# Scores of the plain block placed directly behind it, in layer one of a two-layer graph attention

## The chip, the cores and the metric

The kernel runs on one core of one Trainium2 chip. The core has a matrix engine (TensorE, PE in the profile, its weight loads PEld), VectorE (DVE), ScalarE (ACT), GpSimd (POOL), and DMA queues, of which most here are issued by SyncE (SP). The metric is the time on the device of one execution, as the median of several.

## The reference, cut to what matters

```python
h = jnp.maximum(_layernorm(x, axis=-1), 0.0)          # x: (128, 64, 768)
for l in range(2):
    m_left  = einsum('bsh,oh->bso', h, W_left[l])
    m_right = einsum('bsh,oh->bso', h, W_right[l])
    u_left  = einsum('bih,bjh->bij', h, m_left) / sqrt(768)
    u_right = einsum('bih,bjh->bij', h, m_right) / sqrt(768)
    u = u_left * triu(adj) + u_right * swapaxes(triu(adj, 1), 1, 2)
    e = exp(u) * adj
    attention = e / (sum(e, axis=2) + 1e-10)
    ctx = attention @ (einsum('bsh,oh->bso', h, W_lin[l]) + b_lin[l])
    h = relu((ctx - mean) / (std + 1e-3) * ln_a[l] + ln_b[l])
return x + h
```

All matrices are 32-bit floats. What matters here are `m_left` and `m_right` (six blocks of 256 output columns in all, each a sum over three blocks of 256 input columns) and the scores, the products of `h` with them inside each batch of 64 tokens.

## The kernel before, in words

The 8192 tokens are cut into 32 parts of 256 tokens (four batches of 64). Each layer has two passes: `pass_one` makes `m_left`, `m_right`, the scores and the softmax, `pass_two` the rest. Only layer one's `pass_one` (in the code `l == 0`) is touched.

That pass starts with the **plain block**: parts 0 and 1, whose 12 output blocks (six per part) are made as 12 chains of three block products each, 36 in all. Behind it come the **superblocks** of three parts each (`SUPER[1]`, `SUPER[2]`, ...). A superblock needs only 40 block products (`PRODUCTS`, L116) for its 54 plain ones, by a bilinear scheme: each product multiplies a sum of weight blocks (`W_OPS`, L142) with a sum of token blocks (`T_OPS`, L133), and its result is added into several output blocks (`READS`, L122). Sums of weights are made once, while the plain block runs, on VectorE and GpSimd; sums of tokens are made anew for each superblock, on GpSimd. I call a weight sum W followed by its number in `W_OPS`, a token sum T followed by its number in `T_OPS`, and the first superblock's products 0, 1, 2, ... as they stand in `PRODUCTS`. Products 0, 1, 3, 4, 5, 6 and 7 take the token sums T9, T12, T16, T17, T19, T21 and T23.

A block product (`product`, L691) is four matmuls of 128x128 on 256 columns, which the profile lists as eight records. Its output fills one PSUM bank of 512 columns. Four banks take turns (`bank_of`): C, D, X, Y in the plain block and in the first superblock. There are six such banks (Z and V are the others), and two more, `sc`, that hold scores.

**Output of the plain block.** When a chain ends, ScalarE copies its bank into the output tile (L889): even chains belong to part 0 (tile `m0`), odd ones to part 1 (`m1`). The last four copies (chains 8 to 11) are, by bank, C, D, X and Y; chain 10 completes `m0`, and chain 11 `m1`.

**Staging.** While the plain block is emitted, `weights.stage` is a list of PSUM banks. A weight sum on VectorE first has one operand copied by ScalarE into the next bank of that list (L517), and then reads that bank and one SBUF tile (L522 or L245). The list is a ring: a bank can be filled again when the sum that read it has ended. In the first superblock the list is empty, and sums read SBUF alone. The copies of L517 and L889 share ScalarE's queue in the order in which they are emitted.

**Scores.** `scores(k)` (L722) makes the scores of superblock k: for each pair of batches q (two per part), for each of the six channel blocks c, four small matmuls; 96 matmuls or 192 records for the plain block. The first half reads `m0`, the second `m1`. Its output for the plain block is the first of the two `sc` banks, which is also the third bank of the staging ring. In the superblock behind it, it is emitted after product 3. The reads of products 0 to 3 overwrite the same `m` tiles and so come behind it.

**Softmax.** `softmax(k)` gives eight steps, put into the plan three slots apart (a product has two slots): masks on GpSimd (L745, tile `wm`), then VectorE work that reads the scores (L755), an exponential on ScalarE, and at last a transpose and eight DMAs of SP's queue (L778).

All engines work through their own queue in the order of emission. `turn_of(slot)` runs what the plan holds for a slot and emits sums by a planner's clock that counts slots, not microseconds.

Of the kernel before, what the change touches and what calls it, by code (L numbers as in the profile page):

```python
# [17 lines left out]
def kernel(  # L18
# [48 lines left out]
    def put(slot, *fs):  # L67
        plan.setdefault(slot, []).extend(fs)

    def put_all(slot, fs, step=1):  # L70
        for f in fs:
            if f is not None:
                put(slot, f)
            slot += step
        return slot
# [99 lines left out]
    SCORED = 3  # L175

    def begins(k, l=0):
        return 0 if k == 0 else 2 * (len(PRODUCTS) if l else PLAIN) + 2 * len(PRODUCTS) * (k - 1)
# [142 lines left out]
    KEEP = {}  # L321
# [333 lines left out]
    def pass_one(l, start, final):  # L655
        with tc.tile_pool(name=f"one{l}", bufs=2, reuse_waits="tile") as sp, \
# [34 lines left out]
            def product(bank, w, ts, new, slot, n=TH):  # L691
                p = bank[:, :2 * n].rearrange("p (g n) -> p g n", g=2)
                for g in range(2):
                    for c in range(K2):
                        at = 0
                        for t in ts:
                            t = t[:, c]
                            n = math.prod(t.shape[1:])
                            o = p[:, g, at:at + n]
                            if len(t.shape) == 3:  # L700
                                o = o.rearrange("p (b s) -> p b s", b=t.shape[1])
                            nc.tensor.matmul(o, w[:, c, g * P:(g + 1) * P], t,  # L702
                                             start=(new and g == c == at == 0), stop=(c == K2 - 1),
                                             skip_group_check=True)
                            at += n
                    if g == 0:
                        turn_of(slot)

            def out_of(bank, thirds=False, o=0):
                if thirds:  # L710
                    p = bank[:, :4 * CUT].rearrange("p (g b s) -> p g b s", g=2, s=WIDE)
                    return p[:, :, :, THIRDS[o // 6][1]:]
                return bank.rearrange("p (g b s) -> p g b s", g=2, s=S)

            def into(o, thirds=False):
                v, k, i = o // 6, o // 3 % 2, o % 3
                if thirds:
                    r, n = THIRDS[v]
                    return both[:, i * K2:(i + 1) * K2, :, k, r + n:r + WIDE]
                return M[v][:, i * K2:(i + 1) * K2, :, k, :]  # L720

            def scores(k):  # L722
                nq = 2 * len(SUPER[k])
                p = KEEP["scores"].rearrange("p a (q m) -> p (a q) m", m=P)
                for q in range(nq):
                    ht, m = HT[1, l, SUPER[k][q // 2]], M[q // 2]
                    for c in range(C):
                        for h in range(PAIR):
                            b = q % 2 * PAIR + h
                            mb = both[:, c, q // 2 * PB + b] if l and k == 0 else m[:, c, b]  # L730
                            mb = mb.rearrange("p k j -> p (k j)")
                            for e in (0, 32):
                                nc.tensor.matmul(p[h * S + e:h * S + e + 32, q, e:e + 95],  # L733
                                                 ht[:, c, b * S + e:b * S + e + 32], mb[:, e:e + 95],
                                                 start=(c == 0), stop=(c == C - 1))
# [45 lines left out]
            def softmax(k):  # L781
                CHAIN[k] = chain(k)
                return [lambda: next(CHAIN[k], None)] * 8

            mid = None
            if l == 0:
# [18 lines left out]
                def mid():  # L805
                    for f in turns[1:]:
                        f()
                    load_rows(0, 1, sp)
                    load_rows(0, 2, other)
                    for t in range(2):  # L810
                        nc.sync.dma_start(KEPT[0][t], HT[1, 0, t])
                    load_adj(0)
                    cols.extend([column("a_col", ln_a[0]), column("b_col", ln_b[0])])
# [8 lines left out]
            def bank_of(n):  # L822
                n %= BANKS
                return KEEP["CD"][n] if n < 2 else KEEP["XYZV"[n - 2]]

            weights, tokens = Weights(() if l else W_OPS, 2, True), TOKENS[l]
# [5 lines left out]
            def turn_of(slot):  # L832
                now = slot * 0.86 if l == 0 or slot >= 80 else slot * 0.6 + 20.8
                clock["vector"] = max(clock["vector"], now - 1.0) + sum(getattr(f, "vector", 0.0) for f in plan.get(slot, ()))
                run(slot)
                if fetch and slot >= start["weights"] and slot % 3 and free:
                    fetch.popleft()()
                if weights.left and slot >= start["weights"]:
                    while clock["vector"] <= now and weights.some(nc.vector):
                        clock["vector"] += 0.62  # L840
                    if clock["pool"] <= now and start["pool"] <= slot < start["tokens"]:
                        if weights.some(nc.gpsimd, 40):
                            clock["pool"] = max(clock["pool"], now) + 1.35
                if clock["pool"] <= now + 1.5 and tokens.step(slot):
                    clock["pool"] = max(clock["pool"], now) + 1.35
# [32 lines left out]
            slot = 0  # L878
            for n, (w, t) in enumerate(order):
                bank = bank_of(n % CHAINS)  # L880
                for j in range(3):
                    tok = HT[1, l, t][:, j * K2:(j + 1) * K2, :]
                    product(bank, weights.at[3 * w + j], [tok], j == 0, slot)
                    weights.used(3 * w + j)
                    if j == 2:
                        if n == 0 and mid:
                            mid()
                            weights.stage = [KEEP["Z"], KEEP["V"], KEEP["scores"][:, 0]]
                        nc.scalar.copy(into(6 * t + w), out_of(bank))  # L889
                    turn_of(slot + 1)  # L890
                    slot += 2
            weights.stage = []

            last = len(SUPER) - 1
            for k in range(FIRST_OF[l], len(SUPER)):
                assert slot == begins(k, l)
                if k:
                    put_all(slot + 2 * SCORED + 4, softmax(k - 1), 3)
                    put(slot + 2 * SCORED + 42, lambda k=k: load_adj(k, nc.scalar))
                if k == last:  # L900
                    final(slot, tokens)
                seen, waiting = set(), []

                def reads(i):
                    for o, c in READS[i]:
                        bank = out_of(bank_of(CHAINS * (k - 1) + i % CHAINS), k == 0, o)
                        to = into(o, k == 0)
                        if o not in seen:
                            seen.add(o)
                            nc.scalar.activation(to, bank, AF.Copy, scale=float(c))  # L910
                        elif abs(c) == 1:
                            added(nc.vector, to, "+" if c > 0 else "-", to, bank)
                        else:
                            nc.vector.scalar_tensor_tensor(to, bank, float(c), to, op0=ALU.mult, op1=ALU.add)  # L914

                for i, (f, t) in enumerate(PRODUCTS):
                    while l and f not in weights.at:
                        fetch.popleft()()
                    w, tok = weights.need(f), tokens.need(k, t)
                    product(bank_of(CHAINS * (k - 1) + i % CHAINS), w, tok, i < CHAINS, slot, TH if k else 2 * CUT)  # L920
                    tokens.used(k, t)
                    if k == last:
                        weights.used(f)
                    waiting.append(i)
                    if i == SCORED and k:
                        scores(k - 1)
                    if i >= SCORED or k == 0:
                        for n in waiting:
                            reads(n)
                        waiting = []  # L930
                    turn_of(slot + 1)
                    slot += 2
# [432 lines left out]
```

## Time and profile before

| | us |
|---|---|
| median of 3 runs | 2652.43 |
| lowest and highest | 2652.22, 2653.41 |
| the profiled execution | 2648.42 |
| its span, first to last instruction | 2646.6 |

TensorE was granted a mean of 0.995 of its full clock in the profiled execution. The plain block starts 11.18 us after the span's start, and the first superblock's product 0 at 77.08 us. In a timeline, a row gives the start, the duration, the engine, the line, the operation, the tiles (out<-in), how many instructions are merged, and in brackets how long the engine sat idle before and which instruction ended that.

### The profile page before, as it was taken

The numbers are of one execution on the slowest core, as the hardware profiler recorded it, in microseconds if no ns is written. First come the engines' busy times: TensorE is split into PE (matmuls) and PEld (weight loads), VectorE is DVE, ScalarE is ACT, GpSimd is POOL, SyncE is SP. The second block draws the span as 40 slices with busy tenths as digits, with TensorE's granted clock in tenths as the row PEclk, the third lists the DMA queues.
The fourth block names the chain that finished last, engine by engine and source line by source line (L and its number), as shares of the span: only waits on it lengthen the run. The fifth ranks groups of instructions, "written<-read, shape, count | busy, mean of one in ns | idle before, by whom it ended". The sixth has DMA issues, their size and how long they took to land. (4 is left out here: it accounts for less than half of the span.)

```text
span 2646.6 us, 47202 instructions
## 1 busy us (share of the span) xinstructions
PE 2591.6 (98%) x18122; PEld 2217.1 (84%) x18122; DVE 1780.6 (67%) x2888; ACT 935.4 (35%) x1969; POOL 1763.1 (67%) x1392
## 2 busy tenths in 40 slices
PE   9899999999999999999999999999999989999998
PEld 8788888888888888888798888888888878887886
DVE  7878787777768445554456667677666676666667
ACT  5522223223113244454542222122222335555453
POOL 4766676666668657676276666667666657878786
PEclk9999999999999999999999999999999999999999
DMA  7443534343421354445794424253532215555655
GB/s 220 113 111 86 124 93 110 93 119 79 98 60 56 123 156 149 159 139 182 219 282 101 121 68 108 71 129 93 136 98 70 67 49 157 157 167 166 177 161 146
DMA packets 258465, 331.84 MB, mean 125 GB/s; under 512 B 56002, under 2 KB 190402, under 8 KB 258242
## 3 DMA queue, kind: packets, MB, share of 16 engines
q1 hardware_dynamic: 241442, 320.56, 44.3%
q10 hardware_dynamic: 16800, 8.26, 1.2%
q8 instruction: 145, 2.38, 0.4%
q14 instruction: 78, 0.64, 0.1%
HBM read 213.39 MB, written 115.34 MB: 124 GB/s over the span
## 5 line engine op out<-in xcount | busy, mean ns | idle before, releaser
L245 POOL TENSOR_TENSOR g<-ht 128x512 f32<-128x512 f32 (+1 forms) x620 | 785.9, 1279 | 420.8 <-PE Z L702 71.6
L245 POOL TENSOR_TENSOR g<-g,g 128x512 f32<-128x512 f32 (+1 forms) x310 | 397.9, 1291 | 136.7 <-PE C L702 22.0
L245 POOL TENSOR_TENSOR g<-ht,g 128x512 f32<-128x512 f32 (+1 forms) x272 | 346.1, 1282 | 164.8 <-PE Z L702 42.8
L702 PE MATMUL X<-g,g 128*128 128x256 f32 (+1 forms) x1080 | 252.9, 377 | 6.0 <-DVE m L914 6.0
L1006 PE MATMUL Z<-g,g 128*128 128x256 f32 x1024 | 244.1, 380 | 3.5 <-ACT hl L300 3.2
L702 PE MATMUL C<-g,g 128*128 128x256 f32 x1008 | 239.7, 381 | 4.9 <-POOL g L245 2.2
L702 PEld LDWEIGHTS X<-g,g 128*128 128x128 f32 x1080 | 203.0, 191 | 34.8 <-DVE m L914 6.8
L702 PE MATMUL Y<-g,g 128*128 128x256 f32 (+1 forms) x968 | 225.7, 376 | 3.8 <-POOL g L245 3.8
L1006 PEld LDWEIGHTS Z<-g,g 128*128 128x128 f32 x1024 | 191.6, 190 | 35.8 <-issue 4.1
L379 ACT ACTIVATE ht<-ht,b_col,a_col 128x256 f32<-128x256 f32 x384 | 196.1, 591 | 69.0 <-DMA ht<-h 53.8
L702 PEld LDWEIGHTS C<-g,g 128*128 128x128 f32 x1008 | 190.5, 190 | 32.9 <-POOL g L245 3.5
L702 PE MATMUL Z<-g,g 128*128 128x256 f32 (+1 forms) x936 | 217.0, 375 | 0.0
L702 PE MATMUL D<-g,g 128*128 128x256 f32 x880 | 209.8, 381 | 1.8 <-POOL g L245 1.8
L702 PEld LDWEIGHTS Y<-g,g 128*128 128x128 f32 x968 | 182.0, 190 | 27.8 <-POOL g L245 4.2
L702 PE MATMUL V<-g,g 128*128 128x256 f32 (+1 forms) x840 | 194.6, 375 | 3.1 <-POOL g L245 1.6
L702 PEld LDWEIGHTS Z<-g,g 128*128 128x128 f32 x936 | 174.5, 190 | 23.1
L702 PEld LDWEIGHTS D<-g,g 128*128 128x128 f32 x880 | 168.1, 191 | 25.7 <-POOL g L245 2.5
L1006 PE MATMUL X<-g,g 128*128 128x256 f32 x768 | 182.7, 379 | 0.0
L702 PEld LDWEIGHTS V<-g,g 128*128 128x128 f32 x840 | 157.6, 191 | 23.3 <-POOL g L245 1.7
L1206 POOL TENSOR_TENSOR z<-z,b 128x768 f32<-128x768 f32 x62 | 112.7, 1829 | 81.7 <-DVE z L1203 77.2
L245 DVE TENSOR_TENSOR m<-m,Y 128x512 f32<-128x512 f32 (+2 forms) x196 | 126.5, 667 | 58.4 <-ACT m L910 35.7
L245 DVE TENSOR_TENSOR m<-m,D 128x512 f32<-128x512 f32 x180 | 118.2, 677 | 70.0 <-ACT m L910 51.3
(222 smaller groups left out, 4612.0 us busy)
## 6 DMA issues: line engine op xcount, KB each, us to landing
ht<-h SPq DMA_DIRECT2D x126, 768.0 KB, 6.3
h<-xb SPq DMA_DIRECT2D x124, 384.0 KB, 6.6
z<-z SPq DMA_DIRECT2D x128, 192.0 KB, 3.1
x<-z SPq DMA_DIRECT2D x128, 192.0 KB, 5.4
xr<-in_x_dram SPq DMA_DIRECT2D x120, 192.0 KB, 3.8
out_dram<-xr SPq DMA_DIRECT2D x120, 192.0 KB, 2.7
x<-in_x_dram SPq DMA_DIRECT2D x112, 192.0 KB, 5.4
g<-form SPq DMA_DIRECT2D x40, 256.0 KB, 5.6
```

The costliest lines, as they stand in the source:

```text
L245: (eng.tensor_add if sign == "+" else eng.tensor_sub)(o, a, b)
L379: nc.scalar.activation(ht, ht, AF.Relu, bias=cols[1][:, c:c + 1], scale=cols[0][:, c:c + 1])
L702: nc.tensor.matmul(o, w[:, c, g * P:(g + 1) * P], t, start=(new and g == c == at == 0), stop=(c == K2 - 1), skip_group_check=True)
L1006: nc.tensor.matmul(p[:, n], b[t][:, c, r * P:(r + 1) * P], w[s][:, c, :], start=(i in FIRST and i not in PRELOAD and n == c == 0), stop=(c ...
L1206: nc.gpsimd.tensor_add(zs[k], zs[k], rows["b"])
```

## The change

The scores of the plain block are emitted in front of product 0 instead of behind product 3. The reads of products 0 to 3 then follow each product at once. The softmax steps of the plain block start at slot 2 of the superblock instead of slot 10. As the scores' output is the third bank of the staging ring, the ring has only Z and V from chain 8 on. The conditions `l or k > 1` and `l + k` confine all that to layer one's first superblock; layer two and all later superblocks are emitted as before.

```diff
             for n, (w, t) in enumerate(order):
                 bank = bank_of(n % CHAINS)
+                if n == 8:
+                    weights.stage = [KEEP["Z"], KEEP["V"]]
                 for j in range(3):
...
             weights.stage = []
 
+            if not l:
+                scores(0)
             last = len(SUPER) - 1
             for k in range(FIRST_OF[l], len(SUPER)):
                 assert slot == begins(k, l)
                 if k:
-                    put_all(slot + 2 * SCORED + 4, softmax(k - 1), 3)
+                    put_all(slot + (2 * SCORED + 4 if l or k > 1 else 2), softmax(k - 1), 3)
...
                     waiting.append(i)
-                    if i == SCORED and k:
+                    if i == SCORED and l + k > 1:
                         scores(k - 1)
-                    if i >= SCORED or k == 0:
+                    if i >= SCORED or l + k < 2:
                         for n in waiting:
                             reads(n)
                         waiting = []
```

## Prediction

> **What bounds the kernel now.** The page first: TensorE is busy nearly throughout, so what a change of order can give lies in its gaps.
>
> ```profile
> span 2646.6 us, 47202 instructions
> PE 2591.6 (98%) x18122; PEld 2217.1 (84%) x18122; DVE 1780.6 (67%) x2888; ACT 935.4 (35%) x1969; POOL 1763.1 (67%) x1392
> ```
>
> Then the timeline of PE around the place:
>
> ```profile
> 69.55 5.34 PE L702 MATMUL Y<-ht,g 128*128 128x256 f32 x24
> 77.08 2.51 PE L702 MATMUL C<-g,g 128*128 128x256 f32 x8 [2.19 <-POOL g L245]
> 81.39 3.78 PE L702 MATMUL D<-g,g 128*128 128x256 f32 x8 [1.79 <-POOL g L245]
> 84.96 2.03 PE L702 MATMUL X<-g,g 128*128 128x256 f32 x8
> 90.80 2.57 PE L702 MATMUL Y<-g,g 128*128 128x256 f32 x8 [3.80 <-POOL g L245]
> 93.30 5.16 PE L733 MATMUL sc<-m,ht 128*32 128x95 f32 x192
> 99.49 1.97 PE L702 MATMUL C<-g,g 128*128 128x256 f32 x8 [1.04 <-ACT m L910]
> 101.30 1.89 PE L702 MATMUL D<-g,g 128*128 128x256 f32 x8
> 103.02 1.89 PE L702 MATMUL X<-g,g 128*128 128x256 f32 x8
> ```
>
> The last plain chain ends at 69.55 + 5.34 = 74.89. Product 4 starts at 99.49. Between lie products 0 to 3, the scores, and 2.19 + 1.79 + 3.80 + 1.04 = 8.8 us of idle time, most of it spent on token sums of GpSimd. From product 4 on products follow each other every 1.72 us. So the question is when product 4 starts; what it loses or gains there stays to the end, as PE sets the pace behind it.
>
> PE idles because the sums are late, and ScalarE shows by how much:
>
> ```profile
> 59.76 0.57 ACT L517 COPY sc<-g 128x512 f32<-128x512 f32 x1
> 73.99 0.59 ACT L517 COPY sc<-g 128x512 f32<-128x512 f32 x1 [0.23 <-DVE g L245]
> 81.97 0.58 ACT L889 COPY m<-X 128x512 f32<-128x512 f32 x1
> 87.94 0.58 ACT L889 COPY m<-Y 128x512 f32<-128x512 f32 x1
> 88.42 0.59 ACT L517 COPY sc<-g 128x512 f32<-128x512 f32 x1
> ```
>
> The copies of chains 10 and 11 (L889) stand in ScalarE's queue between staging copies, and those wait for VectorE. Chain 11 left PE at 74.89, and its copy starts at 87.94. Before, that is covered: the scores, which need it, come at 93.30. VectorE, which sets this pace, has no gap:
>
> ```profile
> 60.44 0.69 DVE L522 SCALAR_TENSOR_TENSOR g<-sc,g 128x512 f32<-128x512 f32 x1 [0.82 <-ACT sc L517]
> 68.08 0.68 DVE L245 TENSOR_TENSOR g<-Z,g 128x512 f32<-128x512 f32 x1
> 68.68 0.68 DVE L245 TENSOR_TENSOR g<-V,g 128x512 f32<-128x512 f32 x1
> 73.27 0.69 DVE L245 TENSOR_TENSOR g<-sc,g 128x512 f32<-128x512 f32 x1
> 74.09 0.69 DVE L522 SCALAR_TENSOR_TENSOR g<-Z,g 128x512 f32<-128x512 f32 x1
> 89.10 0.68 DVE L245 TENSOR_TENSOR g<-sc,g 128x512 f32<-128x512 f32 x1
> ```
>
> From 68.08 (the first staged sum emitted in chain 8, W77) to 89.10 (the last, W109) there are 33 sums, 32 steps in 21.02 us: 23 steps of 0.60 (68.08 to 68.68) and 9 of some 0.80 (73.27 to 74.09), the latter mostly where a sum reads or overwrites its predecessor's data.
>
> **The ring of two (first step).** With two banks, a bank's round is the sum (0.69), the way to ScalarE (73.27 + 0.69 = 73.96 to 73.99: 0.03), the copy (0.59) and the way back (59.76 + 0.57 = 60.33 to 60.44: 0.11): 1.42 us for two sums, 0.71 each, a little less where L245 reads the bank; I take 0.69. The 9 steps of 0.80 stay; the 23 of 0.60 cost 0.09 more, 2.07 us. Four plain copies hold ScalarE for 0.48 each (87.94 to 88.42), and a ring of two leaves it no lead to hide them; half of that, 1.0, I count. Together 3.0 us. Carried forward sum by sum with the same durations, three banks give the measured 87.94 and two give 84.3 for chain 10's copy and 90.9 for chain 11's, landing 0.58 later at 84.9 and 91.5. Bounds: nothing, if banks always come free in time; and, if each of the 32 steps takes the longest seen here, 0.82, and all four copies count in full, 26.2 + 1.9 - 21.0 = 7.1 us.
>
> **The scores in front (second step).** They need chain 10's copy for the first part and chain 11's for the second. How fine that wait is can be seen behind them:
>
> ```profile
> 98.27 1.08 ACT L910 ACTIVATE m<-C 128x512 f32<-128x512 f32 x2 [9.25 <-PE sc L733]
> ```
>
> This overwrites a middle third of `m1`, and starts before the scores end at 93.30 + 5.16 = 98.46; so waits go by pieces of a tile. Four of the six channel blocks of a batch pair need no late copy, which leaves three stretches: 32 records at once, 96 behind chain 10's copy, 64 behind chain 11's. Were waits by whole tiles, 96 would be behind the last.
>
> PE's clock matters here. These windows are cut where the granted clock (the column behind POOL) changes, 3.41 us apart:
>
> ```profile
> 74.98:78.39 3.41, 1.31 (x6) 1.18 (x7) 3.28 (x6) 2.97 (x6) 3.28 (x3) 1.00 0.98 334
> 78.39:81.80 3.41, 1.61 (x5) 0.82 (x4) 3.20 (x6) 3.32 (x7) 2.54 (x2) 0.50 1.03 239
> 81.80:85.22 3.42, 3.42 (x9) 2.70 (x9) 3.32 (x6) 3.40 (x7) 2.13 (x2) 0.50 1.04 220
> 85.22:88.63 3.41, 1.77 (x8) 1.22 (x7) 3.31 (x7) 3.18 (x7) 0.88 (x2) 1.00 0.48 103
> 88.63:92.04 3.41, 1.25 (x6) 1.12 (x7) 3.41 (x5) 0.39 (x1) 3.33 (x3) 1.00 0.03 7
> 92.04:95.46 3.42, 3.42 (x60) 2.68 (x62) 3.35 (x9) 0.00 (x0) 2.66 (x3) 0.50 0.01 2
> ```
>
> A window with PE busy for 1.31 or 1.25 us is followed by one at half clock, one with 1.77 is not, and a full one restores it. At half clock a product takes 84.96 - 81.39 = 3.57 us, 0.446 a record against 0.216. The scores by clock (the same view, L733 alone):
>
> ```profile
> 93.30:95.46 2.16, 2.16 (x56) 2.16 (x60) 0.50 0.01 4
> 95.46:98.46 3.00, 3.00 (x144) 2.78 (x136) 1.00 0.03 5
> ```
>
> That is 2.16 / 56 = 0.0386 us a record at half clock, and 3.00 / 136 (started there) = 0.0221 at full.
>
> **The sum.** From 74.9, 32 records take 0.7 us. PE then idles to 84.9, and by the windows its clock is halved. 96 records at 0.0386 last to 88.6, which fills a window, so the clock returns. Idle to 91.5; that window is busy for 0.5 us, so half clock comes at 92.04. 64 records: 22 until then, 42 at half, to 93.7. Product 0 runs 3.95 records until 95.46 and the other 4.05 at 0.216, to 96.3. Products 1 to 3 add 3 x 1.73. Product 4 starts at 101.5 against 99.49: **2.0 us later**. Without the ring's 3.0 it would be earlier, and the wait of 1.04 ahead of product 4 is already gone in this sum, since reads now follow each product.
>
> The Trainium skill speaks to this in "TensorE: Matmul & The Clock Gate", section "HAM oscillation — how this bites in real kernels": the throttle returns after gaps in PE's work of over some 3.4 us. By that, the gap from 88.6 to 91.5 would not halve the clock again, and product 4 would start at 91.5 + 64 x 0.0221 + 4 x 1.73 = 99.8. The trace disagrees: gaps of 2.19 and 1.79 us brought half clock at 78.39 and kept it.
>
> **What lies beside.** Rows that bear on the moved work:
>
> ```profile
> 88.13 2.61 POOL L245 TENSOR_TENSOR g<-ht,g 128x512 f32<-128x512 f32 x2 [2.53 <-DVE g L522]
> 97.26 1.43 POOL L745 TENSOR_TENSOR wm<-adj,tri 128x256 f32<-128x256 f32 x2
> ```
>
> T15 and T16 are the two of 88.13: T15's buffer comes free with a late weight sum (W115), so with the ring they end some 2.4 us later, and the masks (L745, 1.43 us), emitted ahead of T16 now, add to that: 90.7 + 2.4 + 1.4 = 94.5. Product 3 starts at 99.8; cover 5.3 us. T17 to T23 follow at some 1.3 each (2.61 / 2), and by that rate stand before their products by 2 us or more.
>
> ```profile
> 92.38 0.64 DVE L522 SCALAR_TENSOR_TENSOR g<-g,g 128x512 f32<-128x512 f32 x1
> 94.11 0.81 DVE L245 TENSOR_TENSOR g<-g,g 128x512 f32<-128x512 f32 x1
> 100.37 0.69 DVE L245 TENSOR_TENSOR m<-m,D 128x512 f32<-128x512 f32 x1 [4.27 <-ACT m L910]
> ```
>
> The moved reads add one wait on VectorE: product 1's read (100.37) now stands ahead of W116 (94.11), which so waits for product 1's end at 98.1 and, with the statistics between them, ends near 101. T21 takes the buffer that W116 frees, and would be there at 102 for product 6 at 105.0. Cover 3 us; beyond it PE waits.
>
> ```profile
> 118.30 5.16 SPq L461 DMA_DIRECT2D h<-xb  x4
> 123.63 9.47 SPq L361 DMA_DIRECT2D x<-in_x_dram  x8
> 133.22 5.73 SPq L778 DMA_DIRECT2D att<-wm  x8
> 139.06 1.00 SPq L368 DMA_DIRECT2D ht<-h  x2
> ```
>
> The eight attention DMAs are emitted eight slots earlier and so pass the stores and loads of 118.30 and 123.63, which come up to 5.7 us later. The load of 139.06 keeps its place, and its tokens are for superblock 2, some (152 - 80) / 2 x 1.73 = 62 us behind product 4, near 164. The softmax's own steps on VectorE and ScalarE come earlier into queues that wait for PE. I cost all this at nothing.
>
> **Against the runs.** In the profiled execution, of 2648.42 us with 2646.6 of span, this gives 2650.4; it is 4.0 below the median of the runs, 2652.43. The forecast is the median plus 2.0: **2654.4 us**. Its own range: 0.4 (clock never halved again) to 4.9 (whole-tile waits 1.2, a worse phase of the windows 0.7, the ring at 4.0), 2652.8 to 2657.3.
>
> **Rivals.**
>
> *The gate stays open* behind the first scores. +0.4, **2652.8 us**. For it: the 1.77 us window kept full clock. Against: 1.25 and 1.31 did not, and 0.5 is less. The page's rule makes the same.
>
> *The ring costs nothing.* Chain 11's copy lands at 88.5, the clock is halved from 88.63 to 92.04, the scores end at 91.0, product 0 at 93.3, product 4 starts at 98.5: -1.0, **2651.4 us**; at full clock throughout 88.5 + 1.4 + 6.9 = 96.8, -2.7. Against it: the copy of 73.99 already waits on its bank with three.
>
> *The scores fill PE's idle time.* If they ran from 74.9 without waiting for copies, product 3 would wait for T16 alone, 90.7 + 1.4 = 92.1, product 4 would start at 93.9: -5.6, **2646.8 us**. Here the change does what its words say. Against it: the copy of 87.94, which the scores truly need.
>
> *The ring stalls fully*, on the slower side: every step at 0.82, 7.1 us. Chain 11's copy is 4.1 later than in my sum, and product 4 with it: +6.1, **2658.5 us**. It passes 0.2% from a copy at 94.2 on. For it: ScalarE's lead is gone, so each wait shows in full; against: the round of 1.42 for two sums, whose parts are all measured.
>
> **How the numbers follow.** The forecast has 0.66, the open gate 0.12, the free ring 0.10, the filled gap 0.03, the stalled ring 0.09. 0.2% is 5.3 us, about what a measurement of this kernel can tell from no change; so the first three are "same" (0.88), the fourth faster, the last slower. The range takes in the free ring's -2.7 and the forecast's own +4.9: 2649.5 to 2657.5.
>
> **What would show it.** Step one: L517 copies alternating Z and V, VectorE's steps near 0.69, and the last L889 copy at 90 to 92. Step two: a few dozen score records near 75, then the rest in two stretches that start 0.6 us behind the copies of X and Y. Clock: 0.50 from 78.39 to near 88.6 and once more behind. No PE wait on GpSimd in products 0 to 7. It is wrong if the last copy comes before 88 or behind 94, if a later product waits on T21, or if PE's waits behind 110 us change by more than a microsecond.

## The result, and the profile after

| | before | after |
|---|---|---|
| median of 19 runs, us | 2651.89 | 2656.98 |
| lowest to highest | 2648.43 to 2653.43 | 2652.93 to 2661.97 |
| span of the profiled execution | 2646.6 | 2652.8 |

The ratio is 1.0021 with a 95% interval of 1.0015 to 1.0027: the change makes the kernel 4 to 7 us slower, at the edge of the 0.2% that the forecast called no change. The forecast was 2.0 us.

The timeline of PE in the changed kernel, at the place (columns as before, the bracket is the idle time ahead and what ended it):

```profile
69.96 5.34 PE L702 MATMUL Y<-ht,g 128*128 128x256 f32 x24
75.24 0.86 PE L733 MATMUL sc<-m,ht 128*32 128x95 f32 x32
85.37 3.41 PE L733 MATMUL sc<-m,ht 128*32 128x95 f32 x96 [9.27 <-ACT m L891]
91.81 2.76 PE L733 MATMUL sc<-m,ht 128*32 128x95 f32 x64 [3.03 <-ACT m L891]
94.50 2.13 PE L702 MATMUL C<-g,g 128*128 128x256 f32 x8
...
101.64 1.89 PE L702 MATMUL C<-g,g 128*128 128x256 f32 x8
...
120.03 1.97 PE L702 MATMUL X<-g,g 128*128 128x256 f32 x8 [0.96 <-DVE m L918]
...
146.63 1.99 PE L702 MATMUL D<-ht,g 128*128 128x256 f32 x8 [0.46 <-DVE m L245]
...
151.27 2.00 PE L702 MATMUL Y<-ht,g 128*128 128x256 f32 x8 [0.92 <-DVE m L245]
153.74 1.97 PE L702 MATMUL C<-g,g 128*128 128x256 f32 x8 [0.47 <-DVE m L245]
```

The scores run in the three stretches of 32, 96 and 64 records that the prediction drew. Product 4 starts at 101.64. But behind it stand waits of PE on VectorE that the kernel before has not: at product 14 (120.03) and at products 29 (146.63), 31 (151.27) and 32 (153.74); the expectations below call the latter the waits at products 28 to 31. The rows of the kernel before at products 14 and 32 have no wait:

```profile
116.84 1.89 PE L702 MATMUL X<-g,g 128*128 128x256 f32 x8
...
147.92 1.89 PE L702 MATMUL C<-g,g 128*128 128x256 f32 x8
```

So the superblock falls into three stretches. Times are taken from the plain block's end, 75.30 us after and 74.89 before, since the two executions differ by 0.4 us there already:

| stretch, us | before | after | difference |
|---|---|---|---|
| end of the plain block to product 4 | 24.6 | 26.3 | +1.7 |
| product 4 to product 14 | 17.3 | 18.4 | +1.1 |
| product 14 to product 32 | 31.1 | 33.7 | +2.6 |
| sum | 73.0 | 78.4 | +5.4 |

**First stretch.** ScalarE's timeline shows the ring of two, Z and V alone, with waits for VectorE, and the last two copies of the plain block:

```profile
75.21 0.59 ACT L517 COPY Z<-g 128x512 f32<-128x512 f32 x1 [0.23 <-DVE g L245]
76.03 0.59 ACT L517 COPY V<-g 128x512 f32<-128x512 f32 x1 [0.23 <-DVE g L522]
...
84.74 0.58 ACT L891 COPY m<-X 128x512 f32<-128x512 f32 x1
...
91.18 0.58 ACT L891 COPY m<-Y 128x512 f32<-128x512 f32 x1
```

The last copy starts 15.9 us behind the plain block's end (91.18 - 75.30), where it was 13.0 (87.94 - 74.89). How much of that is the ring can be read without PE, from chain 7's copy, which is the last plain copy ahead of the staging copies that the shorter ring changes. Here it is before the change and after it:

```profile
65.73 0.58 ACT L889 COPY m<-Y 128x512 f32<-128x512 f32 x1
```

```profile
66.22 0.58 ACT L891 COPY m<-Y 128x512 f32<-128x512 f32 x1
```

From there to the last copy it takes 22.21 us before (65.73 to 87.94) and 24.96 after (66.22 to 91.18), so the ring of two costs 2.7 us. Against the plain block's end, chain 7's copy itself moves from one execution to the next, from 9.8 to 6.4 us ahead of it in the profiles of this document, and the last copy moves with it.

PE's clock, by windows cut where it changes (the column behind POOL's is the granted clock):

```profile
77.74:81.16 3.42, 0.00 (x0) 0.00 (x0) 2.87 (x5) 3.10 (x6) 3.34 (x4) 1.00 0.89 272
81.16:84.57 3.41, 0.00 (x0) 0.00 (x0) 3.14 (x6) 2.82 (x6) 0.74 (x1) 0.50 1.03 207
84.57:87.98 3.41, 2.61 (x68) 2.61 (x72) 3.08 (x6) 3.00 (x7) 2.52 (x2) 0.50 0.86 181
87.98:91.40 3.42, 0.79 (x36) 0.58 (x28) 3.20 (x6) 3.04 (x6) 0.64 (x1) 1.00 0.11 28
91.40:94.81 3.41, 3.00 (x65) 2.73 (x66) 3.10 (x5) 0.84 (x2) 3.41 (x4) 0.50 0.00 0
```

Half clock twice, behind the long gap and behind the short one.

**Second stretch.** ScalarE's queue after, and below it the same reads and the same exponential before:

```profile
108.55 1.95 ACT L412 ACTIVATE x<-x,nb,rs 128x768 f32<-128x768 f32 x2 [2.39 <-DVE nb L406]
110.51 1.28 ACT L761 ACT_TABLE_LOAD   x1
111.80 0.42 ACT L761 ACTIVATE adj<-adj 128x256 f32<-128x256 f32 x1
112.13 0.58 ACT L914 ACTIVATE m<-Y 128x512 f32<-128x512 f32 x1
```

```profile
106.68 0.60 ACT L910 ACTIVATE m<-Y 128x512 f32<-128x512 f32 x1 [0.95 <-PE Y L702]
...
112.47 1.28 ACT L761 ACT_TABLE_LOAD   x1
```

Product 7's first read (m<-Y) had to wait for PE alone before. After, it stands behind a normalization, a table load of 1.28 us and the exponential. VectorE's read of the same product waits for it, and product 10's read (119.21) behind that comes too late for product 14, which needs its bank. Ahead of product 10's read VectorE now also does its own next softmax steps (L763 to L769), 3.8 us in all, which stood behind that read before:

```profile
112.74 0.69 DVE L245 TENSOR_TENSOR m<-m,Y 128x512 f32<-128x512 f32 x1 [3.30 <-ACT m L914]
...
119.21 0.68 DVE L918 SCALAR_TENSOR_TENSOR m<-X,m 128x512 f32<-128x512 f32 x1
```

**Third stretch.** SP's queue after, then VectorE's timeline:

```profile
121.58 5.16 SPq L778 DMA_DIRECT2D att<-wm  x8
126.84 5.39 SPq L461 DMA_DIRECT2D h<-xb  x4
132.33 6.84 SPq L361 DMA_DIRECT2D x<-in_x_dram  x8
139.27 0.96 SPq L368 DMA_DIRECT2D ht<-h  x2
```

```profile
137.58 0.69 DVE L245 TENSOR_TENSOR m<-m,Y 128x512 f32<-128x512 f32 x1 [0.44 <-PE Y L702]
141.68 1.02 DVE L336 BATCH_NORM_STATS2 st<-x 128x6 f32<-128x384 f32 x2 [3.42 <-DMA x<-in_x_dram]
```

The attention DMAs (L778) hold the issue queue for 5.2 us ahead of the loads of x, which start at 132.33 instead of 123.63 (57.0 us behind the plain block's end instead of 48.7). VectorE's row statistics need them, wait 3.42 us, and hold up all reads behind them in VectorE's queue; products 29, 31 and 32 wait for those reads. Before, the same statistics had no wait:

```profile
134.91 1.01 DVE L336 BATCH_NORM_STATS2 st<-x 128x6 f32<-128x384 f32 x2
```

### The profile page after: what moved, and what is told of

The parts are those of the page before. It is cut to its first block, busy times and chain, and to the rows that moved or that the text cites. A ratio compares the mean times of both kernels' runs of the same rounds, so it can differ in the third digit from the quotient of the medians.

```text
span 2652.8 us, 47193 instructions
## 1 busy us (share of the span) xinstructions
PE 2590.5 (98%) x18122; PEld 2217.6 (84%) x18122; DVE 1782.7 (67%) x2888; ACT 936.0 (35%) x1969; POOL 1761.9 (66%) x1392
## 5 line engine op out<-in xcount | busy, mean ns | idle before, releaser
L733 PE MATMUL sc<-m,ht 128*32 128x95 f32 x6144 | 142.4, 249 | 25.8 <-ACT m L891 12.3
```

What stands on the lines that cost most here:

```text
L733: nc.tensor.matmul(p[h * S + e:h * S + e + 32, q, e:e + 95], ht[:, c, b * S + e:b * S + e + 32], mb[:, e:e + 95], start=(c == 0), stop=(c ...
```

## The experiments

Each is given with its difference from the kernel named. The table comes first, with the three stretches of each profile as above (product starts less the plain block's end), and the ratio of times to the kernel before.

| kernel | to product 4 | 4 to 14 | 14 to 32 | ratio, 95% interval |
|---|---|---|---|---|
| before | 24.6 | 17.3 | 31.1 | |
| after | 26.3 | 18.4 | 33.7 | 1.0021 (1.0015 to 1.0027) |
| softmax late | 28.0 | 17.3 | 31.1 | 1.0003 (0.9994 to 1.0012) |
| DMAs late | 26.2 | 18.4 | 31.2 | 1.0007 (0.9998 to 1.0016) |
| exponential late | 27.3 | 17.3 | 31.1 | 1.0005 (0.9996 to 1.0014) |
| ring of three | 28.0 | 18.4 | 32.6 | 1.0029 (1.0018 to 1.0040) |
| ring of three, softmax late | 30.5 | 17.3 | 31.1 | 1.0006 (0.9997 to 1.0014) |
| ring from chain 11, softmax late | 23.1 | 17.3 | 31.1 | 0.9990 (0.9981 to 0.9998) |
| before, ring of two | 28.5 | 17.3 | 31.1 | 1.0006 (0.9997 to 1.0016) |
| before, scores behind product 2 | 19.5 | 21.0 | 31.1 | 0.9990 (0.9981 to 0.9998) |
| the same, softmax from slot 16 | 18.4 | 21.6 | 31.1 | 0.9992 (0.9983 to 1.0001) |

A stretch comes from one profiled execution, a ratio from 7 to 19 runs. The first stretch moves by a microsecond or two between executions, with the phase of the clock's windows and with chain 7's copy. The other two agree to 0.1 us wherever the edit leaves them alone, but for the third of the ring of three (32.6 where the changed kernel has 33.7). From chain 7's copy to the last one it takes 24.94 to 24.96 us in all five profiles with a ring of two from chain 8, 22.21 to 22.22 in the three with a ring of three, and 23.71 to 23.72 in the three where the ring is cut at chain 11.

**Softmax late** (from the changed kernel):

```diff
-                    put_all(slot + (2 * SCORED + 4 if l or k > 1 else 2), softmax(k - 1), 3)
+                    put_all(slot + 2 * SCORED + 4, softmax(k - 1), 3)
```

> The changed kernel with the softmax steps back at slot 10; scores in front and the ring of two stay. Theory A (of the 5.1 us, the scores in front cost 1.7 and the earlier softmax the rest: some 1.1 where ScalarE's exponential stands ahead of a read, some 2.3 where SP's attention DMAs stand ahead of the loads of x): product 4 still starts 26.3 us behind the plain block, no wait of PE at products 14 and 28 to 31, 1.5 to 2 us over the kernel before. Theory B (all of it follows from the late scores and VectorE's backlog behind them, wherever the softmax stands): the waits stay, 4 to 5 us over the kernel before.

Both late stretches are as before the change, and so is the time, within its interval (0.8 us over, -1.6 to +3.2 with 0.0001 as 0.27 us). Theory B's 4 to 5 us lie outside. Product 4 missed its number, 28.0 instead of 26.3. The last copy came 0.5 us later here against the plain block's end (16.3 instead of 15.9), and the other 1.2 us are the clock's: in this execution the windows lay so that PE stayed at half clock for five of them.

```profile
83.60:87.00 3.40, 1.54 (x40) 1.55 (x44) 3.03 (x5) 2.95 (x6) 1.86 (x2) 0.50 1.02 219
87.00:90.40 3.40, 2.48 (x64) 2.14 (x56) 3.18 (x6) 2.86 (x6) 0.66 (x1) 0.50 0.21 53
90.40:93.90 3.50, 2.00 (x52) 2.00 (x56) 3.13 (x5) 1.93 (x4) 2.97 (x3) 0.50 0.00 0
93.90:97.28 3.38, 3.38 (x26) 2.61 (x19) 1.81 (x5) 0.00 (x0) 2.52 (x2) 0.50 0.00 0
```

The 96 records that filled a window well enough in the changed kernel's profile (2.61 us in 84.57 to 87.98) are split over two here, and neither brings full clock.

**DMAs late** (from the changed kernel; only the last softmax step back at its slot):

```diff
+                    steps = softmax(k - 1)
+                    soon = 7 if l + k < 2 else 0
+                    put_all(slot + 2, steps[:soon], 3)
+                    put_all(slot + 2 * SCORED + 4 + 3 * soon, steps[soon:], 3)
```

> The changed kernel with only the last softmax step (transpose and the eight attention DMAs) at its old slot; the other seven stay early. Theory A: the loads of x start some 5 us earlier than in the changed kernel, the waits at products 28 to 31 (2.3 us) are gone, the wait at product 14 (1.1 us) stays; 2.8 us over the kernel before. Theory B: nothing changes against the changed kernel, 5 us over the kernel before.

The third stretch is back at 31.2, the second stays at 18.4. SP's queue has the old order, and the loads of x start 53.7 us behind the plain block's end (129.40 - 75.74) instead of 57.0. That is 3.3 us earlier where some 5 were expected, as the stores of L461 still start later than before the change (48.3 us behind that end instead of 43.4). VectorE's row statistics wait 0.62 us for the loads instead of 3.42:

```profile
124.07 5.15 SPq L461 DMA_DIRECT2D h<-xb  x4
129.40 9.52 SPq L361 DMA_DIRECT2D x<-in_x_dram  x8
139.03 5.84 SPq L778 DMA_DIRECT2D att<-wm  x8
```

That is theory A's split: the third stretch's 2.6 us come from the attention DMAs' place, and the second's 1.1 us do not.

**Exponential late** (as the last, with 4 in place of 7):

> The changed kernel with softmax steps 1 to 4 (masks, reads of the scores, their sum) early, and 5 to 8 (exponential and behind) at their old slots. Theory A (the exponential with its table load stands ahead of a read of ScalarE's, which makes VectorE's read late on which product 14 waits): product 14 follows product 13 in 1.7 us, where it took 2.9 in the changed kernel and in the one with only the last step late; no wait at products 28 to 31. If it is VectorE's early reads of the scores that make it late, product 14 still takes 2.9.

The second stretch is 17.3: product 14 no longer waits. The early masks and reads of the scores (steps 1 to 4) so cost nothing there, and the 1.1 us come from steps 5 to 7. Product 7's first read starts 1.7 us behind the product's end here (110.74 against 107.16 + 1.89), behind the late normalization alone; in the changed kernel it was 3.4 us (112.13 against 106.82 + 1.89). So the table load and the exponential make up half of that read's delay. But VectorE's steps 6 and 7, which stood ahead of product 10's read, went back with them. Neither was moved alone, so how the 1.1 us divide between the two engines is not shown. The first stretch, 27.3, goes with the last plain copy, which starts 16.8 us behind the plain block's end in this execution (91.51 - 74.67).

**Ring of three** (from the changed kernel):

```diff
-                    weights.stage = [KEEP["Z"], KEEP["V"]]
+                    weights.stage = [KEEP["Z"], KEEP["V"], KEEP["scores"][:, 1]]
```

> The changed kernel with the second scores bank as third bank of the ring from chain 8 on, so that the ring keeps three banks and the scores' own bank is free; all else as changed. Both theories: chain 11's copy 3 us earlier, product 4 some 23.6 us behind the plain block (1 us less than before the change, 2.7 less than changed). Theory A: the waits at products 14 and 28 to 31 stay, together 3.4 us, 2 to 2.5 us over the kernel before. Theory B: they go with the lateness that made them, 0 to 1 us under the kernel before.

The last copy came early as expected, 12.4 us behind the plain block's end. But product 4 came later, not earlier, and the ratio is the highest of all. PE's scores (the view ends at 93 us and so shows 68 of the 192 records), and VectorE's last staged sum:

```profile
90.36 2.92 PE L733 MATMUL sc<-m,ht 128*32 128x95 f32 x68 [14.26 <-DVE g L245]
```

```profile
89.62 0.68 DVE L245 TENSOR_TENSOR g<-sc,g 128x512 f32<-128x512 f32 x1
```

The scores write the first bank of the tile `sc`, the sum reads the second, and the scores wait for it all the same. So product 4 does not tell what the ring costs here, though ScalarE's copies do: with three banks, chain 7's copy to the last takes 22.21 us, as before the change. All 192 records now run in one piece behind the last staged sum. Its late stretches stay long, as theory A has it (18.4 and 32.6 against 17.3 and 31.1).

**Ring of three, softmax late** (both edits):

> Scores in front with a ring of three (the second scores bank as the third) and the softmax at its old slots. Theory A: product 4 some 23.6 us behind the plain block, no wait at products 14 and 28 to 31; 1 us under the kernel before. Theory B: about the same as with the softmax early.

The same wait on `sc`, 17.7 us this time, as the last staged sum came 3.4 us later against the plain block's end in this execution; the late stretches are as before the change. The time is 1.6 us over the kernel before, with an interval across zero. Against the run above with the softmax early the ratios' intervals do not meet (1.0018 to 1.0040 and 0.9997 to 1.0014): the softmax's place again, where theory B had none.

**Ring from chain 11, softmax late** (from the changed kernel):

```diff
-                if n == 8:
+                if n == 11:
                     weights.stage = [KEEP["Z"], KEEP["V"]]
...
-                    put_all(slot + (2 * SCORED + 4 if l or k > 1 else 2), softmax(k - 1), 3)
+                    put_all(slot + 2 * SCORED + 4, softmax(k - 1), 3)
```

> Scores in front, the softmax at its old slots, and the ring cut to two banks only from chain 11 on (before: three banks up to there). The scores still find their bank free, since its last reader is a sum of chain 10. If the ring costs 3 us of the last copy's time: chain 11's copy starts 13 to 14 us behind the plain block's end (15.9 changed, 13.1 before), and product 4 some 24.0 to 25.0 us behind it (26.3 changed, 24.6 before), by the phase of the clock's windows; -0.5 to +0.5 us against the kernel before. If the ring costs nothing, product 4 stays near 26.3 and the time 1 to 2 us over the kernel before.

Here the ring costs 1.5 us instead of 2.7 (23.72 us from chain 7's copy to the last). PE:

```profile
84.20 5.20 PE L733 MATMUL sc<-m,ht 128*32 128x95 f32 x128 [8.84 <-DVE g L522]
90.02 1.51 PE L733 MATMUL sc<-m,ht 128*32 128x95 f32 x64 [0.62 <-ACT m L891]
```

128 records start when the bank's last staged reader ends, and the other 64 follow almost at once, as the last copy starts 14.0 us behind the plain block's end (89.39 against 75.36). Product 4 starts at 23.1, earlier than I expected, since the last 64 records run at 1.51 / 64 = 0.0236 us each, which is full clock, and so do the products behind them. The time is 2.6 us under the kernel before (0.5 to 5.0): with a ring of three up to chain 11 and the softmax left alone, scores in front are faster.

**Before, ring of two** (from the kernel before):

```diff
                 bank = bank_of(n % CHAINS)
+                if n == 8:
+                    weights.stage = [KEEP["Z"], KEEP["V"]]
```

> The kernel before with only the ring of two from chain 8 on; scores and softmax as before. If the ring costs 3 us of VectorE's time in the plain block: chain 11's copy starts near 16 us behind the plain block's end, product 3 (which waits for T16 behind VectorE's sum W115) starts 18.2 us behind it instead of 15.9, product 4 27 instead of 24.6; 2 to 2.5 us over the kernel before. If it costs nothing, all stays.

The last copy starts 17.4 us behind the plain block's end (91.97 - 74.54), against 13.0. Product 3 starts at 19.7 instead of 15.9 and product 4 at 28.5, 3.9 us later; more than the 2.3 and 2.4 expected. Of the last copy's 4.4 us the ring has its 2.7 (24.95 us from chain 7's copy), and 1.7 were there ahead of the cut, as chain 7's copy comes 7.5 us ahead of the plain block's end in this execution instead of 9.2. The row of product 3 shows the wait on GpSimd's T16 grown from 3.80, and half clock in the product itself (3.68 us):

```profile
94.22 3.68 PE L702 MATMUL Y<-g,g 128*128 128x256 f32 x8 [5.06 <-POOL g L245]
```

The time, 1.6 us over, has an interval of -0.8 to +4.2, which holds the stretch's 3.9 and zero.

**Before, scores behind product 2** (from the kernel before):

```diff
+                if n == 11:
+                    weights.stage = [KEEP["Z"], KEEP["V"]]
...
-                    if i == SCORED and k:
+                    at = SCORED if l or k > 1 else 2
+                    if i == at and k:
                         scores(k - 1)
-                    if i >= SCORED or k == 0:
+                    if i >= at or k == 0:
```

> The kernel before with the scores behind product 2 instead of product 3, and the ring cut to two banks from chain 11 on; the softmax as before. The scores then fill PE's wait for T16: they start with chain 11's copy, some 14.5 us behind the plain block's end, product 3 starts near 19.6 and product 4 near 21.4 (24.6 before). T21 and T23 on GpSimd, behind the masks, take back 1 us at products 6 and 7; 2 us under the kernel before.

Product 4 starts at 19.5, 5.1 us earlier than before the change; more than expected, as the scores run while chain 11's copy is still to come. Then PE overtakes GpSimd:

```profile
96.50 1.99 PE L702 MATMUL D<-g,g 128*128 128x256 f32 x8 [0.49 <-POOL g L245]
...
100.32 1.99 PE L702 MATMUL X<-g,g 128*128 128x256 f32 x8 [1.83 <-POOL g L245]
...
102.90 1.99 PE L702 MATMUL Y<-g,g 128*128 128x256 f32 x8 [0.58 <-POOL g L245]
```

The second stretch gives back 3.6 us. What stays is 1.5 us by the stretches, and 2.6 us (0.5 to 5.0) by the runs.

**The same, softmax from slot 16**:

```diff
-                    put_all(slot + 2 * SCORED + 4, softmax(k - 1), 3)
+                    put_all(slot + (2 * SCORED + 4 if l or k > 1 else 16), softmax(k - 1), 3)
```

> Scores behind product 2, the ring of two from chain 11 on, and the softmax steps of the plain block from slot 16 instead of 10, so that the masks come behind T23 on GpSimd. If the masks made products 6 and 7 wait for T21 and T23 (2.4 us in the run with the softmax at slot 10): these waits shrink to under 0.5 us in all, product 13 starts 36 to 37 us behind the plain block (38.7 there, 40.2 before), and the time falls by 2 us more, some 4 us under the kernel before. If the late scores or VectorE made them, product 13 stays near 38.7. A new wait behind the later exponential or the later attention DMAs would show at products 14 to 31.

A miss for the most part. Products 5, 6 and 7 still wait, 1.58, 0.59 and 0.59 us, for token sums, and product 13 starts 38.3 us behind the plain block, not 36 to 37. Each sum takes GpSimd some 1.3 us, and the sums that these products need follow each other without a gap behind T18, which waits for VectorE's weight sum W114:

```profile
94.35 1.27 POOL L245 TENSOR_TENSOR g<-ht 128x512 f32<-128x512 f32 x1 [0.67 <-DVE g L522]
95.70 1.60 POOL L245 TENSOR_TENSOR g<-g,g 128x512 f32<-128x512 f32 x1
97.26 1.27 POOL L245 TENSOR_TENSOR g<-ht 128x512 f32<-128x512 f32 x1
98.61 1.27 POOL L245 TENSOR_TENSOR g<-ht,g 128x512 f32<-128x512 f32 x1
```

T18 starts 18.9 us behind the plain block's end in both runs. With the masks out of the way, T23 ends 27.0 us behind it instead of 28.2, and product 7 starts at 27.1 instead of 28.3: the masks did cost 1.2 us there. The waits stay all the same, since product 4 came 1.1 us earlier too. At their new place the masks then delay the sums of products 9 and 11, which wait 0.27 and 0.24 us, and 0.5 us of the gain is left at product 13. So the bound is GpSimd as a whole, its late start and its pace, and the masks cost something wherever they stand in that row of sums. The time is not to be told from the run above.

## Why the prediction was right, and where its size was off

**The first stretch held.** Forecast: the ring of two delays the last copy by 3.0 us; measured from chain 7's copy, 2.7 (24.96 - 22.21), in each of the five profiles with that ring. Chain 10's copy was drawn 9.4 us behind that end (84.3 - 74.89), and came at 9.4 (84.74 - 75.30). The stretches of 32, 96 and 64 records, and half clock twice, are there. Product 4: 2.0 us later by the forecast, 1.7 measured. The rival in which the ring costs nothing is out by those 2.7 us, the filled gap by the 9.27 us of idle time, the stalled ring by the copy at 91.18, and the gate that stays open by the clock of 0.50 from 91.40.

**What lies beside the scores did not hold, and it is the larger part.** The step that failed is the one that ends with "I cost all this at nothing"; it measured 3.7 us (1.1 + 2.6), so that the sum of the terms is 5.4 instead of 2.0. That 2656.98 us still lies inside the stated range is luck: its upper end was made of waits by whole tiles, a worse phase of the windows and a dearer ring, and none of these made the time.

- The attention DMAs: the prediction saw them pass the stores and the loads of x, and gave their delay as up to 5.7 us. It then asked only about the load of `ht`, whose tokens have 60 us. It did not ask who reads x: row statistics on VectorE, at 141.68, 40 us behind product 4. Nor what stands behind those on VectorE: the reads that free PE's banks. 2.6 us, shown by the run that moves the DMAs back alone.
- The softmax on ScalarE and VectorE: "earlier into queues that wait for PE" was true of the steps' place and wrong of their cost. A table load and an exponential, put ahead of a read of ScalarE's, make that read late and VectorE's read behind it; VectorE's own next steps then stand ahead of the read for which product 14 waits. 1.1 us, gone when steps 5 to 8 go back; how it divides between the two engines stays open.

**The other covers held.** PE does not wait for T16, T21 or T23 in products 0 to 7: the masks ahead of T16 and the wait of W116 behind product 1's read were covered, as forecast. Of the signs by which it would be wrong, the last, waits behind 110 us that change by more than a microsecond, is the one that came.

**What stays open.** The clock's windows and chain 7's copy shift between executions, so a single profile's 1.7 us is one draw, and that it lies so near 2.0 is in part luck; the runs with the same scores and ring give 26.2 to 28.0 to product 4. The totals of single executions hold several microseconds more of such differences far from the change (with the softmax late, the span is 10.9 us longer than before, the stretches 3.3).

## What to carry to other kernels

When a step is moved earlier, follow each of its instructions into its queue, name what it now stands ahead of, and then name the reader of that and what is queued behind the reader; a delay on a DMA queue came back here as a wait of PE, two engines further on. Before filling an idle gap, look what the filler itself waits for: the scores needed a copy that stood 13 us deep in ScalarE's queue, and the bank taken from that queue's ring made it 16. Taking the bank away later (chain 11 instead of chain 8) and leaving the softmax alone turned the same idea from 5 us slower into some 2.6 us faster.

## What the runs showed of the hardware

In these profiles PE's clock goes by how much work falls into each of fixed windows of 3.41 us, more than by the length of a gap. Around the place of the change, a window at full clock with 1.46 us of work or less was followed by half clock in every profile (0.79, 1.25 and 1.31 are in the rows shown), and one with 1.64 us or more was not. A gap of 1.96 us that lay whole in a window brought half clock (the run with the softmax from slot 16), while one of 1.91 us across two windows did not (the run with the scores behind product 2). From half clock back the line is less sharp: windows with 2.48 us and less stayed, those with 2.61 us and more brought full clock, but for one with 2.67 us of block products (82.14 to 85.56 in the run with the scores behind product 2). As the windows lie elsewhere in each execution, the last 64 score records and four products took 11.0 us in one profile (91.90 to 102.91, softmax late) and 9.8 in another (91.81 to 101.64, the changed kernel).

Two banks of one PSUM tile counted as one for PE's wait on VectorE, while the pieces of an SBUF tile did not: the scores into the first `sc` bank waited 14.26 us for a read of the second, and 32 records that read pieces of `m` ran at 75.24, ahead of the last copies into `m0` and `m1`. That is how the program's waits were placed; no run shows it as a limit of the chip.
